# Softening that runs on into the second chunk behind, and evenly placed list products, in a graph attention kernel

## The chip, the cores and the metric

One core of a Trainium2 chip. The metric is device time in microseconds (us) of one launch. Engines: TensorE (PE) multiplies, VectorE (DVE) and ScalarE (ACT) work elementwise, GpSimd (POOL) here issues gathers, SyncE (SP) issues all other DMAs that matter below. Each works through a queue of its own in order.

## What is computed

A graph of N = 2708 nodes with D = 512 features and a symmetric 0/1 adjacency of about 0.6% ones passes four layers, each followed by a residual and a layer norm. Layers 0 and 1 are graph convolutions, layer 3 is a linear convolution of eight heads. The edit lies in layer 2, two attention sublayers one after the other:

```python
def _gat_layer(x, W, adj):
    Wh, Ws = jnp.split(x @ W, 2, axis=-1)
    scores = Wh @ Ws.T
    a = jax.nn.softmax(scores, axis=-1) * adj
    out = a @ Wh
    return jax.nn.leaky_relu(out + x, 0.01)
x = inputs
for l in range(2):
    x = _gat_layer(x, W_stack[l], adj)
```

The softmax runs over all 2708 nodes, so all scores have to be computed in fp32; but after it only some 16 entries of a row survive the product with `adj`, so the second product is a sum over few rows.

## The kernel before

**Staging.** Layers 0 and 1 take 0 to about 590 us of the profiled execution, the attention about 590 to 2050 (the second sublayer's chunks from 1468), layer 3 the rest, with the lists of the last chunk still running in its beginning. Tiles are fp32, 128 x 512 (256 KB). All pages come from one pool of 87 (`PAGES`), tiles for gathers from one of 11 (`WIDES`), PSUM from two sets of four banks. Nothing is reordered by a scheduler: `Ordered` (L54) ties each instruction to the one issued before it on its engine, so the order of the Python calls is each engine's order.

**Chunks.** A sublayer is worked off in six chunks `k` of destination nodes, four of 512 columns, one of 384 and one of 276 (`CH`, L28). A chunk holds 22 row blocks of scores `s` (source nodes, in 128s). Its life has stages, which overlap those of its neighbours:

1. *Scores.* Chunks 0 to 4 form them with a Strassen-Winograd scheme, seven products for two blocks (`pair_steps`, L1695; PSUM tiles `spx`, `spy`; ACT copies them out, DVE adds in `first_block` and `second_block`). `walk` (L2096) yields after each half of such a step: 22 "end" yields, numbered n = 0 to 21, and 20 "mid" yields between them. Chunk 5 forms its blocks one by one (tiles `sp`), 22 "end" yields. `greatest` (L1822) keeps a running maximum `top` on DVE.
2. *Shift.* During the next chunk, at n = 0 to 3: last maxima, transposes, `shift`, the columns' maxima spread over the partitions.
3. *Softening.* `soften` (L1880) is called 26 times (`SOFT` = 22 + 2·2) for a chunk. A call subtracts `shift` from a block (DVE), takes the exponential of the block two calls back (ACT), and adds the block four calls back to `sum`, multiplies it with its mask (both DVE) and stores it to `pairs` in DRAM (SP). In short, a step is three DVE operations, an ACT operation and a store. Masks come four blocks to a DMA (`load_mask`, L1873): two at n = 0 and 1, each later one two masks ahead of its use (L1901).
4. *Lists.* When all 26 calls are made, `fetch` (L1941) lets GpSimd gather, by indirect DMA, rows of `pairs` (a node's features beside its weights) for each list of neighbours; at most ten gathers are out (`AHEAD`). `weigh` (L1993) puts the product of the next list on PE: `acc<-g`, one matmul for a full list or four on quarters of the array for a "quad". Ahead of a chunk's first list stands `den`, the product that adds up `sum`. After the last list of a block comes `end` (L2032) on DVE; in sublayer 1 (the second) also a residual and statistics, and after the chunk's last block a layer norm.

**What sets the order.** `layer` (L2117) walks through the chunks. While chunk k's scores are made, chunk k-1 (`old`) is softened, and chunk k-2's lists are weighed. Before the change a softening step stands at each "mid" from n = 3 and at each even "end" from n = 4: 26 fit exactly into the chunk. At each end up to three lists are weighed. A list is taken only if its gather is due on the code's own clock: `advance` adds each list's PE time, and a gather is due 6 us after a place in a row of gathers 1.15 us apart; for the first gather of a chunk the clock counts 16 us more. `weigh(True)` takes a list even if it isn't due (a *forced* list). The score products advance the clock as well.

**Chunk 5 and behind it.** After the last scores, what is left of chunk 3's lists and the first gathers of chunk 4 are forced with `soften`'s line L1902 (`while ... weigh(True)`) or the loop that waits for `chunks[-3]`; then chunk 5 is softened, with lists and the next stage's work (`fill`: the second sublayer's projections, or layer 3's beginning) in between.

Of the kernel before, what the change touches and what calls it, by code (L numbers as in the profile page):

```python
# [22 lines left out]
NB = 22  # L23
NP = NB * P
DC = D // P
# [460 lines left out]


STREAMED = 4
SOFT = NB + 2 * 2
ALONE = 18  # L490
SEVEN = [k for k in range(len(CH)) if CH[k][1] >= 384]
# [884 lines left out]
class Chunk:  # L1376


    def __init__(self, ly, k):
        self.ly, self.k, self.cw = ly, k, CH[k][1]  # L1380
        self.name = f"{ly.number}_{k}"
        self.blocks = blocks_of(k)
        self.s, self.masks, self.ends = {}, {}, []
        self.half = self.cw // 2
        self.seven = k in SEVEN
        self.part, self.complete, self.ready, self.top = {}, [], [], None
        self.softened = 0
        self.apart = 2 if self.seven else 1
        self.fetched, self.rden = [], None
        self.x, self.first = {}, {}  # L1390
        self.rows = set()
        self.mv = None

        self.to_weigh = []
        for q, (i, _, _) in enumerate(self.blocks):
            ts = lists_of(i)
            self.to_weigh += [(q, t, t is ts[0], t is ts[-1]) for t in ts]
        self.to_fetch = [(q, t) for q, ts, _, _ in self.to_weigh for t in ts]
        self.first_fetch = self.to_fetch[0]
# [9 lines left out]
class Attention:  # L1409
# [7 lines left out]
    def __init__(self, fast):  # L1417
        self.f, self.k, self.nc = fast, fast.k, fast.nc
        self.page, self.bank = fast.page, fast.bank
        tc = self.k.tc  # L1420
        self.scratch = self.k.ctx.enter_context(
            tc.tile_pool(name="pairs", bufs=1, space=DRAM)
        )

        self.pairs = [
            [
                self.scratch.tile([NP, 2 * PAIR + D], FP, tag=f"p{a}{b}", name=f"pairs{a}{b}")
                for b in range(2)  # L1430
            ]
            for a in range(2)
        ]
        self.mixed = self.scratch.tile([DC, P, D], FP, tag="mixed", name="mixed")
        self.quarter = [
            [
                self.scratch.tile(
                    [2, P, pairs_of(k)[0] * P], FP, tag=f"q{a}_{k}", name=f"quarter{a}_{k}"
                )
                for k in range(len(CH))  # L1440
            ]
            for a in range(2)
        ]
        self.sums = [
            [
                self.scratch.tile([3, P, 2, 2 * P], FP, tag=f"u{a}_{k}", name=f"sums{a}_{k}")
                for k in range(STREAMED)
            ]
            for a in range(2)
        ]  # L1450
        self.layers = [AttentionLayer(a, self.pairs[a]) for a in range(2)]
        self.clock, self.fetch_free, self.pending = 0.0, 0.0, []
        self.left = None


    def blank(self):
# [416 lines left out]
    def load_mask(self, ch, g):  # L1873
# [3 lines left out]
        for j in range(j0, j1):  # L1877
            ch.masks[j] = a[:, j - j0, :]

    def soften(self, ch):  # L1880


        nc, v, cw = self.nc, ch.softened, ch.cw
        ch.softened += 1
        if v < NB:
            n = rows_of(v)
            s = ch.s[v][:n, :cw]
            nc.vector.tensor_sub(s, s, ch.shift[:n, :cw])
        j = v - ch.apart
        if 0 <= j < NB:  # L1890
            s = ch.s[j][: rows_of(j), :cw]
            nc.scalar.activation(s, s, AF.Exp)
        j -= ch.apart
        if j < 0:
            return
        if j == NB - 1:
            ch.softened = SOFT
        if j == 0 and ch.k >= 2:
            while self.chunks[ch.k - 2].to_fetch:
                self.weigh(True)  # L1900
        if j % DC == 0 and j + 2 * DC < NB:  # L1901
            self.load_mask(ch, j // DC + 2)  # L1902
        n = rows_of(j)
        s = ch.s[j][:n, :cw]
        if j == 0:
            ch.sum = self.page(f"sum{ch.name}")
            nc.vector.tensor_copy(ch.sum[:, :cw], s)
        else:
            nc.vector.tensor_add(ch.sum[:n, :cw], ch.sum[:n, :cw], s)
        nc.vector.tensor_mul(s, s, ch.masks.pop(j)[:n, :cw])  # L1910
        to = ch.ly.pairs[ch.k % 2][j * P : j * P + n, :]
        if cw == BANK:
            nc.sync.dma_start(
                to[:, : 2 * PAIR].rearrange("j (r x) -> j r x", x=PAIR)[:, :, D:],
                ch.s[j][:n, :].rearrange("j (r x) -> j r x", x=2 * P),
            )
            return
        for r in range(2):
            w = min(2 * P, cw - r * 2 * P)
            nc.sync.dma_start(  # L1920
                to[:, r * PAIR + D : r * PAIR + D + w],
                ch.s[j][:n, r * 2 * P : r * 2 * P + w],
            )
# [17 lines left out]
    def fetch(self, ch):  # L1941


        q, t = ch.to_fetch.pop(0)
        g = self.f.wide(f"g{ch.name}_{q}_{t}")
        i, _, w = ch.blocks[q]

        for b in (q, q + 1):
            self.load_rows(ch, b)

        h = t // ONLY if t < QUARTERS * ONLY else (QUARTERS - 1, 0)[q % 2]
        first, width = (D + P + h * QW, D + P - h * QW) if q % 2 else (0, D + (h + 1) * QW)
        self.nc.gpsimd.indirect_dma_start(
            out=g[:, :width],
            out_offset=None,
            in_=ch.ly.pairs[ch.k % 2][:, :],
            in_offset=bass.IndirectOffsetOnAxis(ap=self.k.givers[:, i, t : t + 1], axis=0),
            element_offset=(q // 2) * PAIR + first,
        )

        begin = max(self.fetch_free, self.clock + (16 if (q, t) == ch.first_fetch else 0))
        self.fetch_free = begin + 1.15
        ch.fetched.append((g, self.fetch_free + 6))

# [28 lines left out]
    def weigh(self, wait=False):  # L1993

        nc = self.nc
        self.fetch_ahead()
        ch = next((c for c in self.chunks if c.to_weigh), None)
        if ch is None:
            return False
        q, ts, first, last = ch.to_weigh[0]  # L2000
        if len(ch.fetched) < len(ts):
            return False
        if ch.fetched[len(ts) - 1][1] > self.clock and not wait:
            return False
        ch.to_weigh.pop(0)
        if ch.rden is None:
            self.divisor(ch)
        w = ch.blocks[q][2]
        gs = [ch.fetched.pop(0)[0] for _ in ts]
        if first:  # L2010
            ch.acc = self.bank(1, f"acc{ch.name}_{q}")
            if ch.ly.number == 1:
                ch.first[q] = self.page(f"x1{ch.name}_{q}")
                self.nc.sync.dma_start(ch.first[q][:w], self.k.saved[1][ch.blocks[q][0]][:w])
        for h, g in enumerate(gs):
            lo, m = (0, w) if len(gs) == 1 else (h * QW, QW)
            e, z = (0, P - lo) if q % 2 else (D + lo, 0)
            nc.tensor.matmul(
                ch.acc[lo : lo + m],
                g[:, e : e + m],  # L2020
                g[:, z : z + D],
                start=first,
                stop=last,
            )
        self.advance(cost(D) if len(gs) == 1 else 1.1)
        if last:
            a = (ch, q, ch.acc, ch.x.pop(q), ch.first.pop(q, None))
            self.later(1.5, lambda: self.end(*a))
        self.fetch_ahead()
        return True  # L2030
# [86 lines left out]
    def layer(self, ly, chunks, fill):  # L2117
        f = self.f
        self.chunks, self.made = chunks, {}
        for k, ch in enumerate(chunks):  # L2120
            old = chunks[k - 1] if k else None
            following = chunks[k + 1] if k + 1 < len(chunks) else None

            n = -1
            for what in self.walk(ch):
                if what == "mid":
                    if old and n >= 3 and old.softened < SOFT:
                        self.soften(old)
                    continue
                n += 1  # L2130
                if old and n < 2:
                    self.load_mask(old, n)
                    self.greatest(old, last=n == 1)
                if old and n >= 4:
                    for _ in range(n % 2 == 0 if ch.seven else 1 + n % 2):
                        if old.softened < SOFT:
                            self.soften(old)
                f.beat()
                if n == 14 and k:
                    f.packed(k - 1)  # L2140
# [10 lines left out]
                        self.restore(ly, i)  # L2151
                self.greatest(ch)

                for _ in range(3):
                    if not self.weigh():
                        break
                if old and n == 2:
                    self.shift_rows(old)
                if old and n == 3:
                    self.shift_columns(old)  # L2160
            assert not old or old.softened == SOFT
        last = chunks[-1]
        self.load_mask(last, 0)
        self.load_mask(last, 1)
        self.greatest(last, last=True)
        self.until(self.clock + 3, fill)
        self.shift_rows(last)
# [119 lines left out]
```

## Time and profile before

| what | value |
|---|---|
| median of 3 runs | 2363.23 us (2360.31 to 2371.82) |
| profiled execution | 2341.13 us |
| its span in the trace | 2339.0 us |
| mean granted PE clock | 0.985 |
| PE busy | 2237.2 us, 96% |
| DVE busy | 1547.5 us, 66% |
| ACT busy | 725.9 us, 31% |
| POOL busy | 717.8 us, 31% |
| gathers | 510 |
| DMA in all | 523.27 MB, mean 224 GB/s |

Where PE is named busy, its work counts; where it is idle, a row says what ended the wait. "issue" stands for a wait that nothing in the profile shows. In a row of the timeline the time in square brackets is the idle time ahead of the operation and what ended it. The starts of the chunks, read from the first score product of each, in us:

| sublayer | chunk 0 | 1 | 2 | 3 | 4 | 5 |
|---|---|---|---|---|---|---|
| first | 761.5 | 829.4 | 900.8 | 1005.0 | 1107.2 | 1184.2 |
| second | 1467.6 | 1532.2 | 1605.8 | 1710.8 | 1813.3 | 1888.9 |

And the last softening product (`s<-s,a`) of each chunk beside the first `den`:

| | chunk 0 | 1 | 2 | 3 | 4 | 5 |
|---|---|---|---|---|---|---|
| first: last product | 908.84 | 1006.85 | 1107.41 | 1187.94 | 1248.6 | 1319.6 |
| first: den | 931.9 | 1037.7 | 1140.3 | 1220.8 | 1306.3 | 1373.0 |
| second: last product | 1611.45 | 1709.73 | 1812.28 | 1893.44 | 1965.38 | 2068.2 |
| second: den | 1633.1 | 1736.2 | 1841.5 | 1923.8 | 2000.8 | 2100.3 |

### The profile page before, as it was taken

What the parts mean: (1) busy time and instruction counts of PE and PEld (TensorE: products, weight loads), DVE (VectorE), ACT (ScalarE), POOL (GpSimd) and SP (SyncE); (2) the same over time, 40 slices, a digit from 0 to 9 for tenths busy, and PEclk for the clock granted to TensorE, in tenths of its full rate; (3) what the DMA queues carried; (4) which work ended last, traced back from release to release, by engine and by line L of the source; (5) the groups of instructions that cost most, each with busy time, mean ns of one, the idle gap of its engine ahead of it and who ended that gap; (6) DMA issues with size and microseconds to landing.
All of it is one profiled execution on the core that took longest, in us unless ns stands there. A gap on an engine that the chain in (4) does not pass through costs nothing.

```text
span 2339.0 us, 29486 instructions
## 1 busy us (share of the span) xinstructions
PE 2237.2 (96%) x9724; PEld 1515.8 (65%) x9724; DVE 1547.5 (66%) x3180; ACT 725.9 (31%) x1654; POOL 717.8 (31%) x827
## 2 busy tenths in 40 slices
PE   9999999999999998999999999998998997899997
PEld 6776876777545786566764345787565763466685
DVE  6777787777655679778784512579888896354523
ACT  7444452222111243233332101243233332251221
POOL 2433521111000002635566450002634564643000
PEclk9999999999999999999999999999999998999999
DMA  9966752223576426968899998426978899884311
GB/s 346 283 186 189 205 148 76 79 77 115 194 262 253 157 77 205 335 218 318 293 362 360 341 399 333 169 78 210 330 243 286 307 306 343 265 249 148 110 47 42
DMA packets 285139, 523.27 MB, mean 224 GB/s; under 512 B 42926, under 2 KB 134758, under 8 KB 284976
## 3 DMA queue, kind: packets, MB, share of 16 engines
q1 hardware_dynamic: 216320, 306.34, 37.9%
q0 software_dynamic: 68656, 214.96, 27.6%
q8 instruction: 78, 1.28, 0.2%
q14 instruction: 85, 0.70, 0.1%
HBM read 335.34 MB, written 185.83 MB: 223 GB/s over the span
## 4 chain that ended last, share of the span: by engine, by line
PE 71%; DVE 13%; issue 6%; DMA 6%; ACT 2%; POOL 1%; SPq 1%; another core or an unknown queue 0%; DVEq 0%; ACTq 0%; POOLq 0%
PE acc L71 27%; PE spx L71 10%; PE mm L71 8%; PE spy L71 8%; PE z L71 6%; PE wst L71 6%; DVE s L71 5%; PE sp L71 3%; DVE sum L71 2%; DMA at<-in_adj_t 1%; DVE top L71 1%; DMA g<-pairs,givers 1%; DMA x<-in_x 1%; DMA x<-x 1%; DVE r L71 1%
## 5 line engine op out<-in xcount | busy, mean ns | idle before, releaser
L71 POOL DMA_INDIRECT g<-pairs,givers x510 | 535.8, 1051 | 912.5 <-issue 359.3
L71 PE MATMUL acc<-m,xh 128*128 128x512 f32 (+4 forms) x1584 | 566.1, 379 | 8.4 <-issue 7.0
L71 PE MATMUL acc<-m,xl 128*128 128x512 f32 (+4 forms) x1584 | 549.5, 365 | 11.0 <-DVE xl L71 9.4
L71 PEld LDWEIGHTS acc<-m,xh 128*128 128x128 f32 (+1 forms) x1584 | 288.1, 188 | 71.9 <-issue 28.6
L71 PEld LDWEIGHTS acc<-m,xl 128*128 128x128 f32 (+1 forms) x1584 | 288.3, 188 | 54.7 <-DVE xl L71 10.4
L71 PE MATMUL acc<-g 128*32 128x512 f32 (+1 forms) x1020 | 285.0, 610 | 12.2 <-DMA g<-pairs,givers 7.5
L71 PE MATMUL mm<-w,ht 128*128 128x512 f32 (+1 forms) x528 | 223.3, 593 | 0.0
L71 ACT CAST m<-at 128x512 fp32r<-128x512 uint8 (+5 forms) x396 | 199.1, 567 | 40.2 <-DMA at<-mask 20.1
L71 PE MATMUL spx<-xs,wst_sb 128*128 128x256 f32 (+1 forms) x800 | 201.3, 375 | 9.2 <-DVE s L71 9.1
L71 PEld LDWEIGHTS spx<-xs,wst_sb 128*128 128x128 f32 x800 | 149.3, 193 | 47.2 <-issue 14.8
L71 DVE TENSOR_TENSOR s<-s,shift 128x512 f32<-128x512 f32 (+3 forms) x264 | 162.4, 619 | 24.7 <-ACT shift L71 14.4
L71 ACT ACTIVATE s<-s 128x512 f32<-128x512 f32 (+3 forms) x264 | 152.0, 582 | 84.8 <-DVE s L71 74.7
L71 DVE TENSOR_TENSOR s<-s,a 128x512 f32<-128x512 f32 (+3 forms) x264 | 166.0, 629 | 18.5 <-issue 9.5
L71 PEld LDWEIGHTS acc<-g 128*32 128x32 f32 (+1 forms) x1020 | 79.7, 136 | 148.5 <-issue 107.4
L71 PEld LDWEIGHTS mm<-w,ht 128*128 128x128 f32 (+1 forms) x528 | 95.8, 186 | 116.6 <-issue 112.3
L71 ACT COPY s<-spx 128x256 f32<-128x256 f32 (+1 forms) x300 | 106.0, 361 | 196.0 <-PE spx L71 143.5
L71 DVE TENSOR_TENSOR sum<-sum,s 128x512 f32<-128x512 f32 (+4 forms) x252 | 156.3, 620 | 4.1 <-ACT s L71 4.1
L71 DVE TENSOR_TENSOR top<-top,s 128x512 f32<-128x512 f32 (+4 forms) x240 | 149.6, 623 | 13.7 <-ACT s L71 9.6
L71 PE MATMUL z<-w,xt 128*128 128x512 f32 (+1 forms) x352 | 151.4, 596 | 0.0
L71 PE MATMUL wst<-xt,mixed 128*128 128x512 f32 (+2 forms) x384 | 150.9, 545 | 0.0
L71 PE MATMUL spy<-xs,wst_sb 128*128 128x256 f32 (+1 forms) x480 | 121.9, 377 | 9.4 <-DVE s L71 9.2
L71 PE MATMUL sp<-xs,wst_sb 128*128 128x276 f32 (+5 forms) x512 | 129.1, 460 | 0.0
(190 smaller groups left out, 2686.3 us busy)
## 6 DMA issues: line engine op xcount, KB each, us to landing
pairs<-z_sb SPq DMA_DIRECT2D x84, 768.0 KB
pairs<-s SPq DMA_DIRECT2D x168, 256.0 KB
s<-sums SPq DMA_DIRECT2D x96, 256.0 KB
at<-in_adj_t SPq DMA_DIRECT2D x84, 256.0 KB
xres<-x POOLq DMA_DIRECT2D x44, 256.0 KB
x<-o POOLq DMA_DIRECT2D x43, 256.0 KB
pairs<-s SPq DMA_DIRECT2D x84, 128.0 KB
a<-mask SPq DMA_DIRECT2D x40, 256.0 KB
```

The source lines that it names most:

```text
L71: ins = call(*args, **kw)
```

## The change

It adds and removes no operation of the result; it moves calls.

- `soften_next` takes its chunk from a queue `to_soften`. A chunk enters the queue after its shift (n = 3), and its softening may run on beyond the chunk's end into the first steps of the chunk behind. Rate in chunks 0 to 4: at each "mid" and each third "end"; in chunk 5: one or two at each end, now from n = 0.
- `FIRST_LANDS`: the clock counts 5 us instead of 16 ahead of the first gather of a chunk.
- `SPACING`: while chunks 2, 3 and 4's scores are made, lists stand at least 1.2, 1.2 and 1.1 us apart on the clock (`next_list`, with up to 4 us of credit), two per end instead of three, and one may also be taken at each "mid".
- `masks_ahead`: for chunks 4 and 5 masks are loaded five groups ahead instead of two; chunk 5's first ones before its scores end.

```diff
+FIRST_LANDS = 5
+SPACING = {2: 1.2, 3: 1.2, 4: 1.1}
...
+        self.masks_ahead = 2 if k < STREAMED else 5
...
+    def soften_next(self):
+        if self.to_soften:
+            self.soften(self.to_soften[0])
+            if self.to_soften[0].softened == SOFT:
+                self.to_soften.pop(0)
...
-        if j % DC == 0 and j + 2 * DC < NB:
-            self.load_mask(ch, j // DC + 2)
+        if j % DC == 0 and j + ch.masks_ahead * DC < NB:
+            self.load_mask(ch, j // DC + ch.masks_ahead)
...
-        begin = max(self.fetch_free, self.clock + (16 if (q, t) == ch.first_fetch else 0))
+        begin = max(self.fetch_free, self.clock + (FIRST_LANDS if (q, t) == ch.first_fetch else 0))
...
+        if self.spacing and not wait:
+            if self.clock < self.next_list:
+                return False
+            self.next_list = max(self.next_list, self.clock - 4) + self.spacing * len(ts)
...
+            self.spacing = SPACING.get(k, 0.0)
             for what in self.walk(ch):
                 if what == "mid":
-                    if old and n >= 3 and old.softened < SOFT:
-                        self.soften(old)
+                    self.soften_next()
+                    self.weigh()
                     continue
                 n += 1
+                if old and n < old.masks_ahead:
+                    self.load_mask(old, n)
+                if not following and n > NB - 1 - ch.masks_ahead:
+                    self.load_mask(ch, n - NB + ch.masks_ahead)
                 if old and n < 2:
-                    self.load_mask(old, n)
                     self.greatest(old, last=n == 1)
-                if old and n >= 4:
-                    for _ in range(n % 2 == 0 if ch.seven else 1 + n % 2):
-                        if old.softened < SOFT:
-                            self.soften(old)
+                for _ in range(n % 3 == 0 if ch.seven else 1 + n % 2):
+                    self.soften_next()
...
-                for _ in range(3):
+                for _ in range(2 if self.spacing else 3):
                     if not self.weigh():
                         break
...
                 if old and n == 3:
                     self.shift_columns(old)
-            assert not old or old.softened == SOFT
+                    self.to_soften.append(old)
+        assert not self.to_soften
+        self.spacing = 0.0
         last = chunks[-1]
-        self.load_mask(last, 0)
-        self.load_mask(last, 1)
```

More of the change, by code (lines that the diff above doesn't have):

```diff
@@ L1453, in __init__ @@
         self.left = None
+        self.spacing, self.next_list = 0.0, 0.0
+        self.to_soften = []
     def blank(self):
```

## Prediction

> **What bounds the kernel now.** I read the busy shares first. TensorE (PE) is busy in 96% of the span, so an edit that only moves instructions can win no more than its idle time and its slow clock.
>
> ```profile
> PE 2237.2 (96%) x9724; PEld 1515.8 (65%) x9724; DVE 1547.5 (66%) x3180; ACT 725.9 (31%) x1654; POOL 717.8 (31%) x827
> ```
>
> All of the edit lies in the attention layers, so I asked for the waits of PE in 755 to 2050 us only (columns: total us, times, longest).
>
> ```profile
> PE spy L71 <- issue: 13.0, 7, 3.8
> PE acc L71 <- issue: 11.0, 16, 7.0
> PE acc L71 <- DVE xl L71: 9.2, 1, 9.2
> PE spy L71 <- DVE s L71: 9.2, 3, 3.5
> PE spx L71 <- DVE s L71: 9.1, 5, 3.8
> PE spx L71 <- ACT v L71: 8.7, 3, 4.7
> PE acc L71 <- DMA g<-pairs,givers: 7.5, 11, 2.4
> PE den L71 <- ACT x2b L71: 5.8, 1, 5.8
> ```
>
> These are not 40 equal waits. The `spy` and `spx` rows are score products kept from a PSUM bank or an operand by a late VectorE (DVE); each is one stall of 2 to 5 us. The timeline at 1703 us (start, duration, engine, operation, idle before it) shows how one arises, at the end of chunk 2 of the second sublayer:
>
> ```profile
> 1704.71 0.65 DVE L71 TENSOR_TENSOR s<-s,spy 128x512 f32<-128x512 f32 x1
> 1705.28 0.68 DVE L71 TENSOR_TENSOR sum<-sum,s 128x512 f32<-128x512 f32 x1
> 1706.00 0.69 DVE L71 TENSOR_TENSOR s<-s,a 128x512 f32<-128x512 f32 x1
> 1706.61 0.16 DVE L71 TENSOR_SCALAR rs_v<-mv 128x4 f32<-128x4 f32 x1
> 1706.80 0.20 ACT L71 ACTIVATE rs_t<-rs_v 128x4 f32<-128x4 f32 x1 [3.74 <-DVE rs_v L71]
> 1706.91 0.35 ACT L71 COPY v<-spx 128x256 f32<-128x256 f32 x1
> 1707.32 2.06 PE L71 MATMUL spx<-t,wst_sb 128*128 128x256 f32 x4 [3.38 <-ACT v L71]
> ```
>
> DVE goes from one operation to the next without a gap, softening steps among them. ScalarE (ACT), whose queue is in order, has a square root that needs DVE's `rs_v`, and the copy that empties PE's bank stands behind it. PE's 3.38 us are DVE's backlog. The four matmuls after it took 2.06 us, against 1.03 for the same four before.
>
> The last view is busy time by stretch (us, then busy us and instructions of PE, PEld, DVE, ACT, POOL, then PE clock, DMA share, GB/s), for chunks 2, 3, 4, 5 and the tail:
>
> ```profile
> 1585.00:1690.00 105.00, 97.36 (x400) 67.41 (x399) 90.17 (x154) 32.27 (x78) 53.24 (x48) 0.95 0.84 284
> 1690.00:1795.00 105.00, 98.38 (x430) 66.58 (x428) 88.25 (x156) 34.50 (x81) 50.67 (x48) 0.98 0.81 283
> 1795.00:1900.00 105.00, 94.17 (x481) 71.13 (x478) 96.07 (x180) 36.42 (x93) 52.42 (x48) 0.98 0.83 292
> 1900.00:1990.00 90.00, 71.51 (x295) 43.02 (x295) 62.44 (x134) 29.84 (x63) 44.99 (x43) 0.91 0.90 318
> 1990.00:2050.00 60.00, 52.09 (x163) 25.95 (x162) 23.21 (x53) 16.30 (x33) 37.22 (x38) 0.97 0.79 254
> ```
>
> DVE is at 84 to 91% while PE is short of full: close rivals. From 1900 us on PE loses 18.5 of 90 and 7.9 of 60 us, and its clock 9% and 3%.
>
> [...] such a stall costs some 2 us more, two to three groups of four at 2.06 instead of 1.03. [...] the trace lands a gather 3.3 to 8.5 us after its issue.
>
> **The change, part by part.** It adds and removes no instruction; everything is order. For the places I followed the order of the program, as the kernel's own clock (`advance`, `until`) sets it, through both versions; times below are the trace's.
>
> *Softening from 26 steps in one chunk to 26 over a chunk and a bit.* A 512-wide step is a subtraction, a sum and a mask product on DVE, starting 0.60, 0.60 and 0.72 apart: 1.93 us. Per pair of blocks (8.2 us of PE: [...]6.0, and 22.5 lists of a tenth, 2.2) DVE had three steps (5.8), two `top` (1.3), the two combinations (0.95) and the ends of lists (1.2): 9.3 us in the second sublayer, 8.6 in the first. After: 2.67 steps, 8.6 and 7.95. So the drift of DVE behind PE shrinks from 1.1 to 0.4 us a pair. Where DVE's lag ended in a PE stall at a chunk's end, 1703.6 (3.4) and 1804.8 (4.7, clock 2 each), 12 us are at stake; I take 10. In chunk 4, 1868.8 (2.9) and two smaller: 4. At the end of chunk 1 (882.8, 906.6, 1585.4, 1611: 14 us) DVE is full in both versions: there are no lists, pair time is 6.0 us of PE against 8.1 of DVE before and 7.4 after, and the same 26 steps stand ahead of chunk 2's third end or so. I take 0.
>
> *Even spacing of the lists (1.2 or 1.1 us each), also at "mid".* Before, lists are taken up to three per end as soon as they are due; a burst of 11 gathers with stores and masks at 1009 to 1022 has PE waiting 3.8 at 1021, and 4.3 at 1120 to 1123. About 11 us with the slow clock; spacing holds the gathers apart by the lists that free their 11 buffers, I take 5. At 977.6, 1680.8 and 1784.3 (4 us each, DMA share 0.93 to 1.0, ACT and DVE having been late together with no visible releaser), 20 us with the clock: I don't know the cause. If crowded DMA, spacing helps; from 0 to 20, I take 6.
>
> *FIRST_LANDS 16 to 5.* It makes the first list due 12.15 us (5 + 1.15 + 6) after the last softening step instead of 23.15. In the trace the last mask product is followed by the first gather's issue in 2.4 to 3.1 us and its landing 3.9 to 6.6 us later: 6.4 to 9.0 in all, plus DVE's lag at that step, 0.6 to 9.7 (four of six under 4). So most first lists are covered, and 0 to 10 us are lost; I take 2. Earlier lists shift the work: chunks 2 and 3's lists end 1.7 us of PE sooner, chunk 4's 10.5 sooner in chunk 5.
>
> *Masks of chunks 4 and 5 five ahead.* Same DMAs, moved up SP's queue past stores. The 9.2 us wait for `xl` comes from this line, 7.50 us in which DVE stood at a mask product:
>
> ```profile
> 1953.34 0.56 DVE L71 TENSOR_TENSOR s<-s,a 128x384 f32<-128x384 f32 x1 [7.50 <-issue]
> ```
>
> Its mask was issued at 1940.7, behind a row store of 1936.9, and landed 12 us later with DMA at 390 to 430 GB/s. All of chunk 4's masks now go out ahead of the first 8 steps. The whole stop of 1949 to 1967 (17.6 us in two waits) hangs on this and on the normalisation queued behind it in DVE.
>
> *The tail.* At the end of chunk 5 the code forces what remains of chunk 3's and 4's lists: 18 before, 12 after. From 1981 to 2024 PE runs at the gathers' pace, 36 at 1.26 us on GpSimd. The six entries fewer are, by their widths, 12 gathers: 15 us less of gathers, less 5.6 of PE work that has to be done elsewhere. Second-sublayer tail in all: 53 us of loss in 1905 to 2050; 7.5 to 9 of mask, 9 of gathers, some of the stop's rest and slow clock: I take 20, from 5 to 30.
>
> *Costs.* Buffers: the 87 pages turn faster, the shortest spans from a store's issue to the reuse of its page fall from 8.6 to 8.0 us of PE work; 3 us. First-sublayer tail: the same 70-odd MB in 183 us of the kernel's clock instead of 218, 370 GB/s instead of 340, against 412 as the best stretch of the trace; DMA waits of 0 to 20, I take 5. SP's queue gets masks ahead of stores by 1 to 2 us: a store that is late delays the first gather; within the 2 above. GpSimd has the same gathers and nothing moved past them.
>
> *Sum:* -10 -4 +0 -5 -6 +2 -20 +3 +5 = -35. The profiled execution took 2341 us (span 2339), so 2306 against it. The median of the runs is 2363, 22 above the profiled one; I put the same difference on it: **2328 us**.
>
> **Rivals.** *A, the waits change their name* (2356, -7). PE is at 96% and DVE near 90%; what is not waited for DVE is waited for gathers, pages or DMA. For it: DMA share 0.81 to 0.90, the gather-bound tail, unexplained stalls. Against it: the mask wait and the fewer forced lists are concrete. Tail gain 10, chunk ends 5, cost 8.
>
> *B, everything works* (2290, -73). Tail 30, chunk ends 14, unexplained 20, bursts 11, costs near 2. For it: total loss in these chunks is about 97 us against PE's nominal, and 53 in the tail. Against it: four causes must vanish at once.
>
> *C, the first lists come before their gathers* (2385, +22). Due 12.15 us after the step, a list whose DVE was 9.7 late (as at 908.8), 2.5 to issue and 6 to land, needs 18.5; PE reaches it some 13.4 after the step, waits 5 and pays 2 of slow clock, behind it all score products in PE's queue: 7 at each of the eight spots, 56, less 34 of gains. It decides from a lag above 4 us at most spots; the trace has that at two of six, and the lower step rate speaks against it.
>
> **How the numbers follow.** Forecast (-20 to -55) 0.60, A 0.22, B 0.10, C 0.08. Within 0.5% is 12 us, what a measurement can hardly tell from none. Faster: forecast, B and a quarter of A, 0.76; same: most of A, 0.15; slower: C and a corner of A, 0.09. The range 2290 to 2362 leaves out half of B, C and A's edge.
>
> **What would show it.** PE's waits on `v` and DVE's `s` at the ends of chunks 2 and 3 gone; no DVE idle of 7 us ahead of `s<-s,a` in chunk 5; fewer gathers in the PE-idle stretch after the last chunk; the time from chunk 5's start to layer 3 shorter by 15 or more. Wrong if the `den` and first `acc` products wait for `sum` or a gather by 4 us or more at many chunks (C), or if the rows <- DMA g and <- issue grow by what the others lose (A).

## The result, and the profile after

The changed kernel is slower: 2375.57 us median (2366.85 to 2390.43, 20 runs) against 2356.71 (2346.54 to 2375.56, 20 runs), ratio 1.0083, 95% interval 1.0064 to 1.0101. The forecast was 2328 us, between 2290 and 2362.

The page of the changed kernel (busy us, share, instructions):

```profile
span 2374.1 us, 29493 instructions
PE 2251.4 (95%) x9724; PEld 1518.5 (64%) x9724; DVE 1551.5 (65%) x3180; ACT 726.9 (31%) x1654; POOL 715.8 (30%) x827
```

It is the same work, and PE has lost more. These are its waits in the attention, 755 to 2085 us (columns as before: total us, times, longest):

```profile
PE tr_top L71 <- DVE top L71: 16.8, 5, 6.3
PE spx L71 <- issue: 13.6, 11, 2.4
PE acc L71 <- DMA g<-pairs,givers: 13.5, 17, 1.7
PE spx L71 <- ACT s L71: 10.8, 4, 5.3
PE tr_mx L71 <- DVE wide L71: 9.5, 8, 1.7
PE spy L71 <- issue: 8.9, 5, 3.3
PE acc L71 <- ACT xh L71: 6.4, 1, 6.4
```

Two of the leading rows before, `spy` and `spx` behind DVE's `s` (18.3 us), are nearly gone (3.8 us are left), and so is `spx` behind ACT's `v` (8.7, now 1.4). In their place stand two rows of transposes, 26.3 us, that had 1.6 us before, an `spx` row behind ACT's `s` that grew from 1.7 to 10.8, and nearly double the waits for gathers (7.5, now 13.5).

By stage, in us from one chunk's first score product to the next one's:

| stage | before | after |
|---|---|---|
| up to chunk 0, first sublayer | 761.5 | 768.8 |
| first sublayer, chunk 1 | 71.4 | 66.6 |
| chunk 2 | 104.2 | 109.6 |
| chunk 3 | 102.2 | 103.3 |
| chunk 4 | 77.0 | 89.0 |
| chunk 5 and tail | 283.4 | 287.6 |
| second sublayer, chunk 1 | 73.6 | 66.7 |
| chunk 2 | 105.0 | 118.5 |
| chunk 3 | 102.5 | 109.3 |
| chunk 4 | 75.6 | 85.1 |
| chunk 5 to the end | 450.1 | 437.1 |

Chunk 0 itself is left out; it takes 67.9 and 64.6 us in both. The first row holds nothing of the change; over the traces of all runs below it lies between 759 and 771 us. The profile of before is also a fast execution, so the two profiles differ by 35 us and the medians by 19. The tail of the second sublayer is 13 us shorter, as hoped, though 4.4 us of that are list products that went to chunk 4. The loss is in chunks 2 to 4.

Two places show how. The first is the start of chunk 2 in the first sublayer (timeline: start, duration, engine, operation, idle before it and its releaser):

```profile
913.18 0.69 DVE L71 TENSOR_TENSOR sum<-sum,s 128x512 f32<-128x512 f32 x1
913.90 0.69 DVE L71 TENSOR_TENSOR s<-s,a 128x512 f32<-128x512 f32 x1
914.51 0.42 DVE L71 TENSOR_TENSOR s<-s,v 128x256 f32<-128x256 f32 x1
914.85 1.41 DVE L71 TENSOR_TENSOR top<-top,s 128x512 f32<-128x512 f32 x2
916.17 0.68 DVE L71 TENSOR_TENSOR sum<-sum,s 128x512 f32<-128x512 f32 x1
918.83 0.69 DVE L71 TENSOR_TENSOR top<-top,s 128x512 f32<-128x512 f32 x1
919.57 1.12 PE L71 MATMUL tr_top<-ident,top 128*128 128x128 f32 x4 [6.28 <-DVE top L71]
```

The last softening steps of chunk 0 (`sum`, `s<-s,a`) now stand here, ahead of the last maximum of chunk 1 (`top`) in DVE's queue, and PE's transpose needs that maximum.

The second is the end of chunk 2 in the second sublayer:

```profile
1730.25 1.28 ACT L71 ACT_TABLE_LOAD   x1
1732.37 0.88 DVE L71 TENSOR_TENSOR t<-xs,t 128x256 f32<-128x256 f32 x2
1735.69 0.69 DVE L71 TENSOR_TENSOR sum<-sum,s 128x512 f32<-128x512 f32 x1
1736.42 0.69 DVE L71 TENSOR_TENSOR s<-s,a 128x512 f32<-128x512 f32 x1
1737.02 0.17 DVE L71 TENSOR_SCALAR rs_v<-mv 128x4 f32<-128x4 f32 x1
1737.22 0.21 ACT L71 ACTIVATE rs_t<-rs_v 128x4 f32<-128x4 f32 x1 [5.69 <-DVE rs_v L71]
1737.33 0.63 ACT L71 COPY s<-spx 128x256 f32<-128x256 f32 x2
1737.74 2.07 PE L71 MATMUL spx<-t,s 128*128 128x256 f32 x4 [5.33 <-ACT s L71]
```

It is the stall of before in a worse form: the six additions that prepare the next chunk (`t<-xs`) and more softening steps stand ahead of `rs_v`, 5.3 us instead of 3.4, and a slow clock comes behind it (0.50 granted from 1735.3 to 1742.1 us, and 2.07 us for four matmuls that take 1.03 at 1731.4).

### The profile page after: what moved, and what is told of

Read it like the earlier page. It is cut to its first block, busy times and chain, and to the rows that moved or that the text cites. A ratio compares the mean times of both kernels' runs of the same rounds, so it can differ in the third digit from the quotient of the medians.

```text
span 2374.1 us, 29493 instructions
## 1 busy us (share of the span) xinstructions
PE 2251.4 (95%) x9724; PEld 1518.5 (64%) x9724; DVE 1551.5 (65%) x3180; ACT 726.9 (31%) x1654; POOL 715.8 (30%) x827
## 4 chain that ended last, share of the span: by engine, by line
PE 72%; DVE 10%; DMA 10%; issue 5%; ACT 1%; SPq 1%; POOL 1%; POOLq 0%; DVEq 0%; ACTq 0%
PE acc L71 28%; PE spx L71 12%; PE spy L71 9%; PE mm L71 8%; PE z L71 6%; PE wst L71 5%; PE sp L71 3%; DVE s L71 3%; DMA at<-in_adj_t 2%; DMA g<-pairs,givers 2%; DMA pairs<-s 2%; DVE sum L71 1%; DVE top L71 1%; SPq L71 1%; DMA mask<-some 1%
## 5 line engine op out<-in xcount | busy, mean ns | idle before, releaser
L71 PE MATMUL acc<-g 128*32 128x512 f32 (+1 forms) x1020 | 295.9, 610 | 17.3 <-DMA g<-pairs,givers 14.3
L71 ACT CAST m<-at 128x512 fp32r<-128x512 uint8 (+5 forms) x396 | 199.3, 569 | 45.8 <-DMA at<-mask 27.6
```

The source lines that it names most:

```text
L71: ins = call(*args, **kw)
```

## Experiments

All are told against runs of the kernel before in the same group, since that kernel takes about 2295 us in some groups and 2357 to 2364 in others. Where two variants ran in different groups (e9 to e15 against the changed kernel, e16 against e6), I compare their ratios to before. Such a comparison is weaker than the intervals say: the changed kernel itself has 1.0083 in one group and 1.0138 in another. To compare stages I subtracted each matmul's usual length (0.216 us for a recorded 256-column matmul, 28 of which, 6.0 us, make a pair of score blocks; 0.43 for a 512-column one; 0.95 for a quad of four lists, whose median in the profile of before is 1.00; and so on) from the time to the next one's start; what is over is *loss*, waits and slow clock together. The table has both sublayers together; each row is one execution, all from groups near 2295. "Tail" is from the last score of chunk 5 to the next sublayer or to the last list. "All" has some 3.4 us of chunk 0 in it too, the same in every row.

| kernel | chunk 1 | 2 | 3 | 4 | 5 | tails | all |
|---|---|---|---|---|---|---|---|
| before (e5) | 12.6 | 22.7 | 13.8 | 10.7 | 4.2 | 49.8 | 117 |
| changed (e6) | 2.0 | 42.9 | 28.1 | 15.9 | 5.4 | 52.4 | 150 |
| spread alone (e1) | 1.9 | 24.3 | 13.4 | 17.0 | 12.6 | 66.3 | 139 |
| spacing alone (e2) | 15.5 | 16.0 | 11.3 | 13.5 | 5.2 | 42.2 | 107 |
| 5 us alone (e3) | 14.2 | 21.2 | 16.2 | 16.0 | 17.9 | 45.5 | 135 |
| changed, 10 us (e16) | 2.0 | 25.4 | 14.3 | 12.2 | 11.8 | 43.2 | 112 |

**Each part alone, on the kernel before.** The four parts of the diff, one at a time.

e1, the spread:

```diff
+                for _ in range(n % 3 == 0 if ch.seven else 1 + n % 2):
+                    self.soften_next()
...
                 if old and n == 3:
                     self.shift_columns(old)
+                    self.to_soften.append(old)
```

> Only the spread of the softening, on the kernel before: lists, first gather's 16 us and masks as before. Theory S (what is left of a chunk's softening stands ahead of the next maxima in DVE's queue, and PE waits for them at the transposes tr_top and tr_mx): slower by 12 to 25 us, with some 20 to 25 us of PE waits on tr_top and tr_mx. Theory L (the evenly placed lists cost it): about the time of before or 5 to 10 us faster, since DVE's lag at the chunks' ends is smaller.

Measured: 2313.11 us, ratio 1.0083 (1.0066 to 1.0099), 15.6 us of waits on `tr_top` and 16.2 on `tr_mx`.

```profile
PE tr_mx L71 <- DVE wide L71: 16.2, 8, 4.0
PE tr_top L71 <- DVE top L71: 15.6, 4, 6.3
```

The number is theory S's, the reason only in part. The loss table shows chunk 1 gaining 10.7 us and chunk 2 giving back 1.6: the waits at the transposes of chunk 2 are those of chunk 1's end, moved. What is lost lies in chunks 4 and 5 and the tails, 31.2 us, of which some 12 are more waits at the transposes of chunks 4 and 5, and 16.5 the tails, into which six lists of each sublayer have slid (53 instead of 47), since the softening ends later.

e2, the spacing (with the test of `next_list`, as in the change):

```diff
+SPACING = {2: 1.2, 3: 1.2, 4: 1.1}
...
                         self.soften(old)
+                    self.weigh()
                     continue
...
-                for _ in range(3):
+                for _ in range(2 if self.spacing else 3):
```

> Only the even placing of lists (1.2, 1.2, 1.1 us apart, two at an end and one at a mid), softening as before. Theory S: no slower than before, 0 to 8 us faster. Theory L: slower by 10 to 20 us, through single waits of 1.5 to 3 us at score products behind a list and waits of acc for gathers.

Measured: 2284.48 us, ratio 0.9954 (0.9937 to 0.9970). Theory L falls: alone, even lists are worth 10.5 us.

e3, the first gather:

```diff
-        begin = max(self.fetch_free, self.clock + (16 if (q, t) == ch.first_fetch else 0))
+        begin = max(self.fetch_free, self.clock + (5 if (q, t) == ch.first_fetch else 0))
```

> Only the first gather counted at 5 us instead of 16. Theories S and L: within 8 us of before. Theory F (first lists stand in PE's queue before their gathers have landed): slower by 10 us or more, with acc waiting for gathers 3 to 6 us at many of the eight chunks.

Measured: 2306.19 us, ratio 1.0048 (1.0029 to 1.0066).

```profile
PE acc L71 <- DMA g<-pairs,givers: 28.2, 18, 9.7
```

Theory F has its 10 us and its waits (7.4 before), but the long ones stand in the tail of the first sublayer (3.3 and 9.7, behind `den` of chunks 4 and 5), not at many chunks.

e4, the masks (with the lines of the change that use `masks_ahead`):

```diff
+        self.masks_ahead = 2 if k < STREAMED else 5
```

> Only the masks of chunks 4 and 5 loaded five ahead. All theories: 5 to 15 us faster, the 7.5 us of DVE at a mask product in chunk 5 of the second sublayer and the 9 us wait for xl behind it gone. If the mask was only one of several things that came late there: within 4 us.

Measured: 2289.68 us, ratio 0.9979 (0.9968 to 0.9991), some 5 us. The wait for `xl` didn't go. This is DVE and PE in the kernel before (trace of e5), and then with the early masks:

```profile
1906.10 0.56 DVE L71 TENSOR_TENSOR s<-s,a 128x384 f32<-128x384 f32 x1 [6.30 <-DMA a<-mask]
1919.68 0.79 PE L71 MATMUL acc<-m,xl 128*128 128x512 f32 x1 [9.21 <-DVE xl L71]
```

```profile
1909.72 0.69 DVE L71 TENSOR_TENSOR r<-r,x 128x512 f32<-128x512 f32 x1 [4.54 <-DMA x<-x]
1917.82 0.79 PE L71 MATMUL acc<-m,xl 128*128 128x512 f32 x1 [11.74 <-DVE xl L71]
```

DVE has its mask, and stands at a residual row `x<-x` instead, which SP issued at 1904.8 among the stores.

The four parts alone make +19, -10, +11 and -5 us, together +15. That is near the +19 of the whole change, so this sum doesn't yet tell whether the parts act on each other.

**The changed kernel with one part changed.** e5 is the kernel before again, for its trace, and e6 the changed kernel.

> The kernel before once more, on the chip of the next three runs, so that their stages can be compared with a trace of the same chip. All theories: the time of before. If the waits of 4 us with no visible releaser at 978, 1681 and 1784 us belong to the chip and not to the order, they are missing here wherever the time is near 2290.

> The changed kernel once more, on the same chip. Theory S (the transposes wait for DVE): slower than before by 0.6 to 1.0%, with 20 to 26 us of waits on tr_top and tr_mx. Theory L (the lists' place): on a chip with fewer unexplained waits the loss shrinks to 0.3% or less.

Measured: 2287.63 us (one run) for e5; 2326.78 for e6, ratio 1.0138 (1.0118 to 1.0157). In e5 the waits of up to 4 us with no visible releaser are missing: they go with the slower groups. The loss of the change doesn't shrink without them, it grows.

e7, softening back at its old places, the other three parts kept:

```diff
-                    self.soften_next()
+                    if old and n >= 3 and old.softened < SOFT:
+                        self.soften(old)
                     self.weigh()
...
-                for _ in range(n % 3 == 0 if ch.seven else 1 + n % 2):
-                    self.soften_next()
+                if old and n >= 4:
+                    for _ in range(n % 2 == 0 if ch.seven else 1 + n % 2):
+                        if old.softened < SOFT:
+                            self.soften(old)
```

> The changed kernel with the softening's old places (all 26 steps inside the chunk); spacing, 5 us for the first gather and early masks stay. Theory S: 10 to 20 us faster than the changed kernel, that is the time of before or better, with no wait on tr_top. Theory F (the 5 us are to blame): as slow as the changed kernel, acc waiting for gathers 20 us or more.

Measured: 2322.53 us, ratio 1.0119 (1.0099 to 1.0139), with 27.6 us of waits for gathers. Theory S falls as the main cause: without the spread it is nearly as slow. Here the interaction is plain: the three parts that are left make -4 us alone and +27 together.

e8, transposes later:

```diff
-                if old and n == 2:
+                if old and n == (4 if ch.seven else 2):
                     self.shift_rows(old)
-                if old and n == 3:
+                if old and n == (5 if ch.seven else 3):
```

> The changed kernel with the two groups of transposes for the shift at n = 4 and 5 instead of 2 and 3 in chunks 1 to 4, so that DVE can work off what is left of the softening first; softening of the chunk then starts and ends some four steps later. Theory S: waits on tr_top and tr_mx fall from over 20 us to under 6, and the time falls by 8 to 18 us against the changed kernel. Theory L or F: within 6 us of it, or slower, since the lists move towards the tail.

Measured: 2310.49 us, ratio 1.0065 (1.0042 to 1.0088), 16 us faster than e6. But PE's waits for DVE only changed their name in chunk 2 of the first sublayer, which lost 16.8 us (16.7 in e6):

```profile
PE spx L71 <- DVE s L71: 25.5, 6, 6.5
PE tr_mx L71 <- DVE wide L71: 5.9, 3, 4.3
```

DVE's backlog is what has to be waited for, whichever PE instruction meets it. The softening also ended later, and all lists with it: the gain lies in chunk 3 and the tail, and in chunk 2 of the second sublayer, so this run doesn't show the transposes to be the cause. That both numbers of theory S came true (16 us, 5.9 us at the transposes) is luck.

**The 5 us.** e9 puts 16 us back into the changed kernel; e10 takes only the spacing out of it.

```diff
-FIRST_LANDS = 5
+FIRST_LANDS = 16
```

> The changed kernel with the first gather counted at 16 us again; spread, spacing and masks stay. Theory F (the early due lists cost most of it): 15 to 30 us faster than the changed kernel (within 0.3% of before), waits of acc for gathers back from 16 to under 9 us and the first sublayer's tail without a den wait. Theory S (the spread costs most of it): within 8 us of the changed kernel or slower, since lists move to the tail as in the run with the spread alone.

```diff
-SPACING = {2: 1.2, 3: 1.2, 4: 1.1}
+SPACING = {}
...
                     self.soften_next()
-                    self.weigh()
```

> The changed kernel without spacing: no 1.2 us, up to three lists at an end and none at a mid. By the sum of the parts measured alone, 10 us slower than the changed kernel. If spacing and the 5 us work against each other (three parts without the spread came to +27 us where their sum is -4), it is 5 to 20 us faster than the changed kernel.

Measured: e9 2346.44 us, ratio 0.9915 (0.9880 to 0.9951): faster than before, and 1.7% (40 us) from the changed kernel's 1.0083 by this one number. e10: 2364.14, ratio 1.0005 (0.9974 to 1.0035), so with 5 us the spacing costs some 18 us, where alone it gained 10. In e9 chunks 2 and 3 of both sublayers lose 47 us, against 87 in the changed kernel of its first profile. The wait at the transposes stays in e9, the gathers' falls:

```profile
PE tr_top L71 <- DVE top L71: 15.4, 3, 6.3
PE acc L71 <- DMA g<-pairs,givers: 7.1, 8, 2.6
```

So it is theory F, but how? Read from the traces, the first list of chunks 0 to 3 comes 11.2 to 14.4 us after the last softening product in e6 (22.4 to 33.7 in e5), and not one of these eight has a wait. I formed two theories: N, that earlier lists move the layer norm's square root to the chunk's end; C, that they leave no cushion of landed gathers for the lists *behind* the first.

e13, the layer norm of chunks 0 and 1 later:

```diff
-                self.later(2, lambda: self.normalize(ch))
+                self.later(2 if ch.k > 1 else 20, lambda: self.normalize(ch))
```

> The changed kernel with the layer norm of chunks 0 and 1 of the second sublayer begun 20 us of the kernel's clock after its last block instead of 2, so that its square root falls behind the next chunk's first transposes. Theory N (the square root at the chunk's end): the stalls of 5.5 and 5.1 us (copies of spx behind rs_t) go, with their slow clock 10 to 15 us faster than the changed kernel. Theory C (no cushion of gathers): within 5 us of the changed kernel.

e14, 10 us:

```diff
-FIRST_LANDS = 5
+FIRST_LANDS = 10
```

> The changed kernel with the first gather counted at 10 us. Theory C: at least half of the loss against 16 us comes back, some 15 to 25 us faster than the changed kernel, waits of acc for gathers under 10 us. Theory N: little changes unless the layer norm leaves the chunk's end: 0 to 8 us.

e15, 5 us in the first sublayer alone:

```diff
-        begin = max(self.fetch_free, self.clock + (FIRST_LANDS if (q, t) == ch.first_fetch else 0))
+        begin = max(self.fetch_free, self.clock + ((5 if ch.ly.number == 0 else 16) if (q, t) == ch.first_fetch else 0))
```

> The changed kernel with 5 us in the first sublayer and 16 in the second. Theory N: 12 to 25 us faster than the changed kernel, chunks 2 and 3 of the second sublayer each about 12 us shorter, the first sublayer as in the changed kernel. Theory C: half of the loss comes back in each sublayer, so 15 to 20 us faster too, but chunks 2 and 3 of the first sublayer stay 6 us longer each than with 16. The two differ in how much the first sublayer's two chunks keep.

Measured: e13 2374.31 us, ratio 1.0047 (1.0027 to 1.0067), some 8.5 us from the changed kernel's ratio, a little under what N forecast, with intervals that together allow 2 to 15 us. Its two stalls are gone, and two waits for `tr_top` of 3.6 and 4.6 us have come at chunks 3 and 4. e14: 2348.30, ratio 0.9932 (0.9904 to 0.9959): 5 us more of the clock give back 1.5 of the 1.7%. That is C's, and more; it takes the square root off the chunk's end too. e15: 2366.94, ratio 1.0022 (1.0000 to 1.0043), 14 us faster; chunks 2 and 3 of the second sublayer lose 27.3 us instead of 52.1, those of the first 36.2 against 35.3: each sublayer pays for itself. The first sublayer has no layer norm, so no square root at its chunks' ends; yet its chunks 2 and 3 lose some 35 us with 5 us (changed kernel) and 22 with 16 (e9). So N can't be the whole. It is there, as the stalls gone in e13 show, and is the smaller part.

**Two interactions**, on the 10 us kernel (e16 is e14 once more, as their base). e17 takes the spacing out as e10 did; e18 softens less in chunk 1:

```diff
-                for _ in range(n % 3 == 0 if ch.seven else 1 + n % 2):
+                for _ in range((n % 3 == 0 and k != 1) if ch.seven else 1 + n % 2):
```

> The changed kernel with 10 us once more, as the base for the next two. All theories: 0.4 to 1.0% faster than before.

> 10 us, and no spacing (no list at a mid, up to three at an end). If spacing hurts only for want of landed gathers, it helps here, and this run is 5 to 12 us slower than the one before. If spacing hurts wherever the softening is spread (its lists fall between DVE's steps), this run is 5 to 15 us faster.

> 10 us, and in chunk 1, which has no lists, softening steps at the mids only, so that some seven more of chunk 0's steps stand in chunk 2. Theory S (the wait at tr_top in chunk 2 is DVE's backlog from chunk 1): the two waits of 6.4 us fall under 3, each with 2 us of slow clock, 8 to 16 us faster than the base if what is moved isn't late again in chunk 2. Rival: DVE is as late in chunk 2 with the moved steps, or the later lists cost as much: within 5 us of the base.

Measured: e16 2289.99 us, ratio 0.9975 (0.9964 to 0.9987), under the 0.4% that e14 let expect. e17: 2302.83, ratio 1.0034 (1.0019 to 1.0049): with landed gathers at hand, the spacing is worth 13 us. Its sign hangs on the cushion, as expected. e18: 2297.16, ratio 1.0020 (1.0002 to 1.0038), 7 us *slower* than e16. The waits on `tr_top` of 6.3 us are gone, so they were DVE's backlog from chunk 1, but now a copy of `spx` is waited for 8.3 us in chunk 2 of the second sublayer, and chunk 4 there loses 16.9 us instead of 10.5:

```profile
PE tr_mx L71 <- DVE wide L71: 14.3, 8, 4.6
PE spx L71 <- ACT s L71: 11.3, 3, 8.3
```

**Better versions.** e11 has spacing and early masks on the kernel before; e12 also loads the residual rows with the first gather of a block instead of with its first list:

```diff
         self.nc.sync.dma_start(ch.x[q][:w], given[i][:w])
+        if ch.ly.number == 1:
+            ch.first[q] = self.page(f"x1{ch.name}_{q}")
+            self.nc.sync.dma_start(ch.first[q][:w], self.k.saved[1][i][:w])
```

> The two parts that helped alone, spacing and early masks, with the softening's old places and 16 us. If the parts add: 0.6 to 0.7% (14 to 16 us) faster than before. If they fill the same holes: 0.4 to 0.5%.

> As the run before, and the rows x of the second sublayer's residual are loaded with a block's first gather and not with its first list. Theory Q (in chunk 5's last steps DVE waits for whatever SP's queue brings late, first the mask, and the row x<-x once the mask is early): the wait of about 10 us for xl and of DVE's r<-r,x go, another 6 to 12 us faster than the run before. Rival (the rows were only the last of many): within 4 us of it.

Measured: e11 2348.41 us, ratio 0.9907 (0.9871 to 0.9943), the lowest of all, though e9, e12 and e14 lie inside its interval; e12 2347.78, ratio 0.9932 (0.9903 to 0.9961). In e12 the wait for `xl` (4.9 us in e11) is gone, the one behind ACT's `m` falls from 11.5 to 8.1, the tail of the second sublayer loses 39.6 us instead of 47.1, and chunks 2 and 3 lose 5 us more: no gain in time. e11 beside e9 shows no gain of the spread on top of spacing and masks; their intervals leave room for some 10 us either way.

**How the cushion works.** These are PE's waits for gathers, 745 to 2080 us, in e6 and in e16:

```profile
PE acc L71 <- DMA g<-pairs,givers: 15.8, 20, 2.1
PE acc L71 <- DMA g<-pairs,givers: 5.3, 10, 1.7
```

They are not the whole, for only a small part of the missing cushion shows as a wait of PE. This is the changed kernel (e6), PE and its weight loads at two lists of chunk 2 in the second sublayer:

```profile
1637.48 1.07 PE L71 MATMUL acc<-g 128*32 128x512 f32 x8
1648.15 2.03 PE L71 MATMUL acc<-g 128*32 128x512 f32 x6
1649.13 0.14 PEld L71 LDWEIGHTS acc<-g 128*32 128x32 f32 x2 [0.84 <-DMA g<-pairs,givers]
```

A quad, eight recorded matmuls, takes 1.07 us. In the second one two weight loads had to wait for late gathers: its first six matmuls count as 2.03 us of busy PE, and the profile shows 0.16 us of PE waiting ahead of the last two, though it was 3.16 us until the next product could start. In chunks 2 and 3 of both sublayers e6 and e16 weigh the same lists, and e6 loses some 17 us more at quads (25.0 against 7.8). The profile's waits of PE for gathers there are only 2.7 us more (3.5 against 0.8).

The chain that ended last says it in one row for each kernel, in 745 to 2100 us, first e6 and then e16:

```profile
by line: PE spx L71 18.2%; PE acc L71 15.9%; PE spy L71 12.9%; DMA g<-pairs,givers 9.7%; PE sp L71 7.0%; PE z L71 6.1%; PE wst L71 5.5%; DVE s L71 4.6%; issue 3.7%; POOL g L71 2.9%; DVE sum L71 1.8%; DVE top L71 1.5%; DMA pairs<-s 1.3%; DVE
```

```profile
by line: PE acc L71 20.9%; PE spx L71 19.7%; PE spy L71 14.2%; PE sp L71 7.1%; DVE s L71 5.2%; PE wst L71 5.0%; PE z L71 4.9%; DMA g<-pairs,givers 2.9%; DMA pairs<-s 2.3%; DVE sum L71 2.3%; issue 2.2%; DVE top L71 1.5%; PE mix L71 1.0%; DMA
```

9.7% of the chain runs through gathers, against 2.9% with 10 us and 5.0% in e5.

The landings in the traces show the stock itself. This is what I count for the lists of chunks 0 to 3 (first row) and 0 to 2 (the others), both sublayers:

| | e6 (5 us) | e16 (10 us) | e5 (before, 16 us) |
|---|---|---|---|
| gathers landed when a chunk's first list starts | 3 or 4 | 6 to 11, once 3 | 11 |
| mean over a chunk's lists | 2.4 to 3.2 | 3.7 to 4.5 | 4.1 to 5.2 |
| median us from a list's last landing to its first matmul | 0.6 to 2.5 | 2.4 to 3.4 | 2.9 to 4.2 |
| lists, of 144, that start less than 1 us after it, or ahead of it | 53 | 27 | 30 |

That e5 begins with eleven and still has 30 such lists fits its bursts of up to three lists at an end, which use the stock up; no run here isolates this.

The rest of the 31 us by which e6 is behind e16 in chunks 2 and 3: the two stalls at the chunks' ends (10.3 us), and some 8 in score products, most of it slow clock by my estimate (granted 0.94 and 0.97 in chunks 2 and 3 of the second sublayer, against 0.97 and 1.00 in e16), less some 4 us that e16 has more at `tr_mx`. The parts overlap, so the sum is an account, not a proof; that 10 us in place of 5 repairs most of it is measured (e14, e16).

## Why the prediction was wrong

**The step that failed** is the one on the first gather: "most first lists are covered, and 0 to 10 us are lost; I take 2". The first lists were covered, all eight in chunks 0 to 3. The price was 11 us alone (e3) and 37 to 40 in company (e6 against e16, the changed kernel against e9, by their ratios). So of the 54 us between the forecast of -35 and the measured +19, some 36 lie in this step, an estimate from these runs. I compared a list's due time with its gather's landing for the *first* list only. The lists behind it go at 1.2 us apart, gathers are issued at 1.26 (1630.73, 1631.99, 1633.25 and 1634.51 us in e6), so a chunk that starts with three or four landed gathers doesn't get more (a mean of 2.4 to 3.2). And I had the spread of landings, 3.3 to 8.5 us, in my hand: a stock of six and more takes in much of it, one of three does not (27 lists start within 1 us of their landing, or ahead of it, in e16, and 53 in e6). Rival C had about the size (+22 forecast, +19 measured) and the right part of the diff, but the wrong mechanism: no first list of chunks 0 to 3 waits, and no lag of DVE is in it. That its size fits is luck. Rival A foresaw the look of the profile, waits that change their name, but at -7 us.

**The spread:** forecast -14. It was right that DVE drifts less in a chunk (the three 512-wide operations of a step take 0.68 to 0.69 us each in the profile of before). Chunk 1's end, where I took 0, gained 10.6 us (12.6 to 2.0 of loss); I take it that the lower drift helped there too. But what is left of a chunk's softening falls on n = 0 to 2 of the next one, which I had not looked at: it had been the place where DVE caught up. The two transposes wait 6.3 us each in chunk 2, and the ends of chunks 2 and 3 of the second sublayer, where I took 10 us of gain, stall for 10.3 in e6 instead of e5's 4.6. e9 against e11 makes the spread about 0 in the end; e1 makes it +19, largely in chunks 4 and 5 and through later lists.

**Spacing:** forecast -11, alone -10.5. Right in size; how much of it is what I named (bursts) I can't say, and the 6 us for the waits with no visible releaser have no basis: in the slower groups they are still there (`spx` and `spy` <- issue: 22.5 us in the profile after, 15.2 before). I had also put these three at 4 us each; the profile's waits there are 3.8, 2.0 and 1.5 us. The interaction with the first gather I didn't see.

**Masks and tail:** forecast -20, of it 7.5 to 9 for the mask. The mask wait went and a row's came in its place; masks alone gave 5 us. The second sublayer's tail lost 36.9 us in e6 against 44.2: 7 us of gain, of which the waits for `xl` and `m` make some 3 (15.0 to 12.0), and what is lost at and inside the lists the rest. The first sublayer's tail lost 9.9 more (15.5 against 5.6), 6.6 of it waits for gathers; I had taken 5 for crowding, an estimate; that crowding is the cause was not shown.

**Not tested:** the 3 us for pages. No wait in the traces points at them.

## What to carry to other kernels

When a consumer is started earlier, ask not only whether its first input is there but how many inputs are ready when it starts: if producer and consumer run at nearly the same pace (1.26 us a gather, 1.2 a list here), that stock is all the protection there ever is. A stretch in which an engine seems idle may be where it catches up; before putting work there, look at who needs it next. And measure the parts of a change in company, not only alone: spacing was worth 10 to 13 us with a stock of landed gathers (e2, e17) and cost some 18 without (e10).

## What of the hardware was not expected

- A group of matmuls in which a later one waits for a gather is recorded as busy in e6: 2.03 us for six against 1.07 for eight. PE's busy share hid this wait. The 2251 us of "busy" against 2237 for the same instructions may come from such waits and from slow clock (mean granted 0.983 against 0.985); the split was not measured.
- After a stall of PE of 5.3 us four matmuls took 2.07 us instead of 1.03. The granted clock is 0.50 from 1735.3 to 1742.1 us, 4.4 us of it after PE had begun again at 1737.7, so this stall cost an estimated 2.2 us beyond itself. The length of a stall alone doesn't tell what follows: in the profile of before the clock is 0.50 from 1809.9 to 1813.2 us after a stall of 4.66 us, a mean 0.54 from 1707.3 to 1711.0 after one of 3.38, and 1.00 from 886.6 to 890.0 after one of 3.47.
- The kernel before takes 2295 us in some groups of runs and 2357 to 2364 in others. The groups of e1 to e8 and e16 to e18, on three chips, are near 2295; those of e9 to e15, all on one other chip, near 2363. The traces differ in waits of score products (`spx`, `spy`) with no visible releaser (up to 3.8 us before, once 6.5 in e11), which stand in every trace of the slower groups and in none of the others. So they go with the group, as far as is on record with the chip, and not with the order of the program; what they are stays open.
